# A step of context keys is dealt only after its staging buffer's last transfers were issued three rounds ago

## The chip, the core and the metric

One core of a Trainium2 chip runs the whole program. The metric is device time in microseconds (us) of one execution. Five engines have queues of their own and work through them in order: TensorE (PE in the profile, its weight loads PEld), VectorE (DVE), ScalarE (ACT), GpSimd (POOL) and SyncE (SP), which here issues nearly all transfers.

## The reference

Two layers of a transformer block work on `x` of shape (4, 512, 320), with a context of shape (4, 1601, 192):

```python
h1 = ln(x);  x = attn(h1, h1)  + x        # self attention, 20 heads of 16
h2 = ln(x);  x = attn(h2, ctx) + x        # cross attention, 1601 keys
h3 = ln(x);  a, g = split(h3 @ ff_w1 + ff_b1)
x = (a * gelu(g)) @ ff_w2 + ff_b2 + x     # 1280 hidden
# attn: softmax(q k' / 4) v, then the output projection wo and its bias
```

All of it is in float32.

## The kernel before

The work is cut into *units*: a batch element and a group of four heads for attention (20 units of self and 20 of cross attention in a layer), and one unit for each batch element of the feed-forward part. A unit of attention goes through its keys in *chunks* of 128: 4 chunks in a self unit, 13 in a cross unit. For a chunk PE makes the scores (`st`, L1187), subtracts the row maximum by one more product (L1190), ACT takes the exponential (L1200), and a chunk later PE multiplies by the values (`av`, L1214). The maxima come from products made ahead for the next unit (`sps`, L1011), which DVE reduces (L1030). Heads sit in slots of 32 rows, so that four small products run side by side in the array.

Beside this stream, filler work is dealt: normalisation, queries, keys, values, output projections, the turning of the context. Each kind has a chain, a queue in the planner's hands; an entry has a cost, a due round, a condition `ready` and a condition `soon`. A chunk is two *rounds* of the planner's clock, and at the end of each chunk the function `steps` takes entries from the heads of the chains, in order of their due rounds, as long as a credit lasts. An entry whose `soon` is false holds up its chain, and the other chains go on. All this happens while the program is built; the chip sees fixed queues.

The keys of the context are made by `keys_of_context(i)`, a *key step*: four PSUM banks (`kps`, L873) are filled by PE, two are copied by ACT and two by DVE (L882) into a staging buffer that lies in the tile `w2` (`w` or `w_109` in the views), POOL splits the result into a high and a low part (L697, L698), and SP issues the transfers that spread it over the rows of `kT` (`kT<-w`, L893 and L889). There are two such staging buffers, `kstage`, used in turn. `slots_soon` queues a step's transfers for the rounds that follow; if a buffer is asked for again before they were issued, `empty` issues them at once. A key step is 24 merged rows of products for one pair of units, or 48 smaller ones for a single unit; there are 80 key steps.

Nothing in the planner asks whether the transfers out of a buffer have gone when the next key step for it is dealt. The copies at L882 then carry that wait in the queues of ACT and DVE.

## Time and profile before

| | us |
|---|---|
| median of 3 runs | 3103.72 (3101.41 to 3106.84) |
| the profiled execution | 3100.62 |
| its span, first to last instruction | 3098.8 |
| PE busy | 2966.7 (96%) |
| DVE busy | 2192.6 (71%) |
| ACT busy | 1963.5 (63%) |
| POOL busy | 1269.3 (41%) |

The span is the stretch in which instructions ran; the execution's own time is 1.8 us longer. Ends of products are modelled, so PE's busy share tells little by itself; the idle time in front of an instruction and the name of what ended it tell more. In the rows of the views, `L882` is line 882 of the kernel, `xN` a count, and in a list of waits stand the total in us, the number of waits and the longest. The mean granted TensorE clock was 0.986 of full speed.

### The profile page before, as it was taken

How to read it: one execution, taken by the hardware profiler on the slowest of the kernel's cores; microseconds unless marked ns; L12 is line 12 of the kernel's file. 1: busy time of each engine (PE TensorE's matmuls, PEld its weight loads, DVE VectorE, ACT ScalarE, POOL GpSimd, SP SyncE). 2: the span in 40 equal slices, each digit the busy share in tenths (PEclk: the TensorE clock that was granted, in tenths of full speed). 3: DMA queues.
4: the chain of work that ended last, by engine and by line, in shares of the span. 5: the costliest groups of instructions: out<-in, count | busy, mean ns of one | idle time of the engine just before them, and what ended most of it. 6: DMA issues, size and time to landing. Idle time of an engine off the chain costs nothing.

```text
span 3098.8 us, 93413 instructions
## 1 busy us (share of the span) xinstructions
PE 2966.7 (96%) x37842; PEld 1615.6 (52%) x37842; DVE 2192.6 (71%) x4315; ACT 1963.5 (63%) x4029; POOL 1269.3 (41%) x1451
## 2 busy tenths in 40 slices
PE   8999999999999999999998999999999999999999
PEld 4455555554554555455554555555555555544555
DVE  7787888778778778522258888888888888884221
ACT  3677568777777778711137775778778778884110
POOL 3445335544544544311125553455555455442000
PEclk9999999999999999999999999999999999999999
DMA  4433221221221221300113332212211221112000
GB/s 104 103 69 80 55 47 41 59 46 34 59 46 33 58 42 22 88 6 1 28 36 84 73 69 48 44 46 42 42 46 35 41 57 35 31 25 67 9 13 13
DMA packets 213064, 145.35 MB, mean 47 GB/s; under 512 B 147476, under 2 KB 182680, under 8 KB 212632
## 3 DMA queue, kind: packets, MB, share of 16 engines
q1 hardware_dynamic: 211752, 138.32, 19.7%
q8 instruction: 297, 4.87, 0.7%
q10 hardware_dynamic: 880, 1.06, 0.1%
q14 instruction: 135, 1.11, 0.1%
HBM read 33.04 MB, written 7.93 MB: 13 GB/s over the span
## 4 chain that ended last, share of the span: by engine, by line
PE 70%; DVE 20%; DMA 2%; issue 2%; POOL 2%; ACT 2%; SPq 1%; ACTq 0%; POOLq 0%; DVEq 0%
PE av L1214 17%; PE st L1187 10%; DVE pm L1030 9%; PE fps L1309 9%; PE sps L1011 9%; PE yps L1364 6%; DVE nmax L1030 5%; PE ops L1126 3%; PE qps L797 3%; PE vps L965 3%; PE st L1190 3%; PE fps L1322 2%; PE kps L873 2%; PE vps L947 1%; DMA kT<-w 1%
## 5 line engine op out<-in xcount | busy, mean ns | idle before, releaser
L1030 DVE TENSOR_REDUCE pm<-sps 128x1 f32<-128x512 f32 x1920 | 1187.0, 679 | 86.1 <-PE sps L1011 79.3
L1011 PE MATMUL sps<-kT,q 32*128 32x512 f32 (+1 forms) x6400 | 1067.2, 406 | 26.5 <-DMA q<-stage 5.5
L1200 ACT ACTIVATE pr<-st 128x512 f32<-128x512 f32 (+1 forms) x1710 | 907.3, 603 | 216.1 <-PE st L1190 205.5
L1187 PE MATMUL st<-q,kT 32*128 32x512 f32 (+1 forms) x5440 | 943.8, 437 | 36.8 <-ACT w L882 27.3
L1231 POOL TENSOR_TENSOR o<-o,pr 128x512 f32<-128x512 f32 x359 | 462.0, 1287 | 694.4 <-ACT pr L1230 678.6
L1187 PEld LDWEIGHTS st<-q,kT 32*128 32x128 f32 (+1 forms) x5440 | 480.5, 181 | 395.6 <-ACT pr L1200 136.3
L1214 PE MATMUL av<-pr,vals 128*32 128x512 f32 (+1 forms) x3420 | 642.9, 614 | 37.6 <-DVE pm L1030 12.4
L1011 PEld LDWEIGHTS sps<-kT,q 32*128 32x128 f32 x6400 | 546.4, 185 | 137.2 <-DVE pm L1030 30.4
L1190 PE MATMUL st<-m,units 32*128 32x512 f32 (+1 forms) x2720 | 534.1, 393 | 2.8 <-DMA m<-turned 2.8
L1200 ACT ACTIVATE wself<-st 128x512 f32<-128x512 f32 (+1 forms) x867 | 464.3, 603 | 87.1 <-PE st L1190 81.5
L1030 DVE TENSOR_REDUCE nmax<-sps 128x1 f32<-128x512 f32 x640 | 395.6, 679 | 103.9 <-PE sps L1011 99.5
L1214 PE MATMUL av<-wself,vals 128*32 128x512 f32 (+1 forms) x1734 | 373.1, 612 | 12.9 <-DVE pm L1030 8.1
L1231 POOL TENSOR_TENSOR o<-o,wself 128x512 f32<-128x512 f32 x191 | 245.2, 1284 | 316.5 <-ACT wself L1230 316.4
L1332 ACT ACTIVATE pr<-fps,b 128x512 f32<-128x512 f32 x80 | 54.8, 687 | 373.5 <-PE fps L1322 266.1
L1309 PE MATMUL fps<-hT,w 128*128 128x512 f32 x640 | 285.0, 597 | 0.0
L1190 PEld LDWEIGHTS st<-m,units 32*128 32x128 f32 (+1 forms) x2720 | 251.4, 182 | 21.9 <-issue 2.7
L1230 ACT COPY pr<-av 128x512 f32<-128x512 f32 x359 | 218.9, 610 | 29.9 <-PE av L1214 29.0
L1214 PEld LDWEIGHTS av<-pr,vals 128*32 128x32 f32 (+1 forms) x3420 | 91.7, 108 | 207.0 <-DVE pm L1030 102.4
L1309 PEld LDWEIGHTS fps<-hT,w 128*128 128x128 f32 x640 | 118.5, 190 | 149.4 <-issue 147.2
L697 POOL TENSOR_SCALAR stage<-stage 128x256 fp32r<-128x256 f32 (+1 forms) x155 | 106.9, 689 | 172.2 <-ACT stage L808 87.5
L873 PEld LDWEIGHTS kps<-ctxT,w 32*128 32x128 f32 (+1 forms) x4992 | 113.6, 160 | 51.6 <-ACT pr L1200 23.1
L500 POOL TENSOR_SCALAR root<-root 128x4 f32<-128x4 f32 x23 | 5.2, 224 | 323.7 <-DVE root L494 323.3
(101 smaller groups left out, 3282.7 us busy)
## 6 DMA issues: line engine op xcount, KB each, us to landing
q<-stage SPq DMA_DIRECT2D x314, 128.0 KB
kT<-w SPq DMA_DIRECT2D x240, 104.0 KB
aT<-o SPq DMA_DIRECT2D x320, 32.0 KB
kT<-stage SPq DMA_DIRECT2D x156, 64.0 KB
kT<-w SPq DMA_DIRECT2D x80, 72.0 KB
w<-in_L_xattn_ff_w_dram SPq DMA_DIRECT2D x20, 256.0 KB
m<-turned SPq DMA_DIRECT2D x318, 4.0 KB
ctxT<-ctxT SPq DMA_DIRECT2D x24, 208.0 KB
```

Of the source, the lines that this page charges most:

```text
L697: eng.tensor_scalar(high.bitcast(F32R), x, 1.0, None, ALU.mult)
L873: see(nc.tensor.matmul(ps[to : to + n, :PIECE], lhsT=wk_q[rows, k, u.g * GD : u.g * GD + n], rhs=first.kvT[rows, k, at : at + PIECE], star ...
L1011: see(nc.tensor.matmul(out, lhsT=u.q[rows, t // 2, e, t % 2 * P : (t % 2 + 1) * P].bitcast(F32R), rhs=u.kT[rows, keys].bitcast(F32R), star ...
L1030: see(nc.vector.tensor_reduce(to[:, j : j + 1], ps, AX.X, ALU.max, negate=(ns == 1)))
L1187: see(nc.tensor.matmul(st[:r, :], lhsT=keys, rhs=u.q[rows, :, e].bitcast(F32R), start=(e == 0), stop=False))
L1190: see(nc.tensor.matmul(st[:r, :], lhsT=units_of[rows, :r].bitcast(F32R), rhs=u.mrow[rows, :].bitcast(F32R), start=False, stop=True,))
L1200: see(nc.scalar.activation(p[:r], st[:r], AF.Exp))
L1214: see(nc.tensor.matmul(ps[j * SLOT : (j + 1) * SLOT, :], lhsT=columns_of[:r, head : head + SLOT], rhs=pr.pop((c, j))[:r, :], start=True, s ...
L1230: see(nc.scalar.copy(vo, ps))
L1231: nc.gpsimd.tensor_tensor(u.o, u.o, vo, ALU.add)
L1309: see(nc.tensor.matmul(ps, lhsT=w1[:, k, i * FF + c * P : i * FF + (c + 1) * P], rhs=u.hT[:, k, :], start=ahead and k == 0, stop=not ahead ...
L1364: see(nc.tensor.matmul(ps[:, :D], lhsT=hid[c][:, t * P : (t + 1) * P], rhs=w2[:, c, :], start=(c == 0), stop=(c == NHC - 1),))
```

## The change

Two lists are added. `asked` counts how often a staging buffer was asked for, and `sent` notes the round in which the last transfer of each step was issued. The new condition `room` holds for a key step when the step before the last one, which used the same buffer, has all its transfers issued and three rounds have gone by. It is given to the key steps of the cross units as their `soon`. The ordinary staging buffer, which queries and the keys of self units use, only keeps count.

```diff
     groups = {"stage": deque(), "kstage": deque()}
+    sent = {"stage": [], "kstage": []}
+    asked = {"stage": 0, "kstage": 0}
+
+    def room(kind):
+        n = asked[kind] - 2
+        return n < 0 or len(sent[kind]) > n and clock["round"] >= sent[kind][n] + 3
...
     def stages(kind="stage"):
         empty(kind, 1)
+        asked[kind] += 1
...
         def last():
             done()
+            sent[kind].append(clock["round"])
...
-                add(chain, 1.1, lambda i=i: keys_of_context(i), keys_due - after, free)
+                add(chain, 1.1, lambda i=i: keys_of_context(i), keys_due - after, free, lambda: room("kstage"))
```

No instruction is added or taken away: the same work stands in another order. Of the 80 key steps, 21 were dealt in the round in which the last transfer out of their buffer was issued, and 5 two rounds after it; now 28 are dealt four rounds after, and none earlier (entries are taken at even rounds here, so three becomes four). The scores, the maxima and the rounds in which they stand do not move. The other filler entries move, since the planner deals them into the places that came free.

The first place is ACT's queue in the first cross unit of the second batch element, in the first layer. The four copies of the two key steps that come first, then the exponentials, then the next key step's copies. Before:

```order
L882 COPY w_109<-kps 128x104 x4
L1200 ACTIVATE wself<-st 128x512 x3
L1200 ACTIVATE pr<-st 128x512
L1230 COPY pr<-av 128x512
L882 COPY w_109<-kps 128x104 x2
L1200 ACTIVATE pr<-st 128x512 x4
L1225 COPY o<-av 128x512
L882 COPY w_109<-kps 128x104 x2
```

In ACT's queue of the new kernel, from the same four copies on (its lines are 8 higher):

```order
L890 COPY w_109<-kps 128x104 x4
L1208 ACTIVATE wself<-st 128x512 x3
L1208 ACTIVATE pr<-st 128x512
L1238 COPY pr<-av 128x512
L1208 ACTIVATE pr<-st 128x512 x4
L1233 COPY o<-av 128x512
L981 COPY vals<-vps 128x12x16 x2
L1208 ACTIVATE pr<-st 128x512
L1208 ACTIVATE wself<-st 128x512 x3
L1238 COPY wself<-av 128x512
L890 COPY w_109<-kps 128x104 x2
```

The third key step's copies moved from one chunk after the first two to three chunks after them.

The second place is PE's queue one batch element later, at the last of the four key steps. Before, the key step (`kps`) is alone between the values (`av`) and the next scores:

```order
L1214 MATMUL av<-pr,vals 32x512 x2
L1214 MATMUL av<-wself,vals 32x512 x2
L873 MATMUL kps<-ctxT,w_107 128x104 x24
L1187 MATMUL st<-q_92,kT_86 128x512 x2
L1011 MATMUL sps<-kT_89,q_93 128x512 x2
```

In PE's queue of the new kernel, two chunks later, a step of queries (`qps`) has come into the same place:

```order
L1222 MATMUL av<-pr,vals 32x512 x4
L881 MATMUL kps<-ctxT,w_107 128x104 x24
L805 MATMUL qps<-hT,w_109 32x128 x12
L1195 MATMUL st<-q_92,kT_86 128x512 x2
L1019 MATMUL sps<-kT_89,q_93 128x512 x2
```

The key step and the queries, which stood in two chunks, now share one. Twelve key steps stand so in the new order, with queries or values beside them that divide the array in another way; over the whole queue PE changes the division 1544 times instead of 1524.

The third place is SP's queue at the first of these places. Before, the transfers of the third key step stand ahead of those of a finished unit's output (`aT<-o`):

```order
L893 DMA kT_87<-w_109 64x4x104 x2
L893 DMA kT_89<-w_109 64x4x104 x2
L893 DMA kT_87<-w_109 64x4x104 x2
L1117 DMA aT<-o 16x512 x4
L893 DMA kT_89<-w_109 64x4x72
```

In SP's queue of the new kernel:

```order
L901 DMA kT_87<-w_109 64x4x104 x2
L1125 DMA aT<-o 16x512 x4
L901 DMA kT_89<-w_109 64x4x104 x2
L901 DMA kT_87<-w_109 64x4x104 x2
L901 DMA kT_89<-w_109 64x4x72
```

The output's transfers now stand ahead of the third key step's; this happens in about ten units.

## The prediction

> **What bounds the kernel now.** I read the page first, then the groups by line for the idle time ahead of each, then the waits of PE and ACT, and last the order of time around one wait.

> ```profile
> span 3098.8 us, 93413 instructions
> PE 2966.7 (96%) x37842; PEld 1615.6 (52%) x37842; DVE 2192.6 (71%) x4315; ACT 1963.5 (63%) x4029; POOL 1269.3 (41%) x1451
> PE 70%; DVE 20%; DMA 2%; issue 2%; POOL 2%; ACT 2%; SPq 1%; ACTq 0%; POOLq 0%; DVEq 0%
> ```

> PE is almost never idle and holds 70% of the chain that ended last: whatever lets PE stand still costs about its own length, and nothing else costs much. PE's idle time in the whole span is 3098.8 - 2966.7 = 132 us. The groups tell where some of it is:

> ```profile
> L1187 PE MATMUL st<-q,kT 32*128 32x512 f32 (+1 forms) x5440 | 943.8, 437 | 36.8 <-ACT w L882 27.3 <-DVE pm L1030 6.6 <-ACT pr L1200 1.5
> L882 DVE COPY w<-kps 128x104 f32<-128x104 f32 x160 | 34.5, 257 | 78.4 <-DMA kT<-w 44.7 <-PE kps L873 32.9
> L882 ACT COPY w<-kps 128x104 f32<-128x104 f32 x160 | 31.5, 249 | 96.6 <-PE kps L873 49.8 <-DMA kT<-w 43.7 <-issue 2.2
> ```

> The score products lose 27.3 us to the copies into the staging buffer, and those copies, short in themselves (249 and 257 ns), wait for the transfers out of it. As waits:

> ```profile
> PE st L1187 <- ACT w L882: 27.3, 15, 2.9
> PE av L1214 <- DVE pm L1030: 20.5, 28, 1.3
> PE st L1187 <- DVE pm L1030: 6.6, 9, 1.3
> PE sps L1011 <- DVE w L882: 4.9, 5, 1.0
> ACT w L882 <- DMA kT<-w: 43.7, 16, 3.8
> ```

> The largest single item of PE's idle time is the first line, and the count of 15 goes with the 16 of the last. One such wait in order of time, at the first place that the change's section shows:

> ```profile
> 634.89 0.39 ACT L882 COPY w<-kps 128x104 f32<-128x104 f32 x2 [0.72 <-PE kps L873]
> 636.82 10.81 SPq L893 DMA_DIRECT2D kT<-w  x12
> 638.48 1.62 PE L873 MATMUL kps<-ctxT,w 32*128 32x104 f32 x47
> 640.39 0.41 PE L1190 MATMUL st<-m,units 32*128 32x512 f32 x2
> 642.66 0.39 ACT L882 COPY w<-kps 128x104 f32<-128x104 f32 x2 [3.10 <-DMA kT<-w]
> 642.96 0.84 PE L1187 MATMUL st<-q,kT 32*128 32x512 f32 x2 [2.16 <-ACT w L882]
> 644.58 1.07 PE L1214 MATMUL av<-wself,vals 128*32 128x512 f32 x3
> 646.38 1.60 PE L873 MATMUL kps<-ctxT,w 32*128 32x104 f32 x48
> 647.74 0.48 PE L1187 MATMUL st<-q,kT 32*128 32x512 f32 x2
> ```

> The buffer is filled at 634.89, its transfers are issued from 636.82 on, and the next key step for the same buffer is on PE at 638.48. ACT reaches that step's copies and stands for 3.10 us until the transfers have landed at 642.66. The exponentials are queued behind the copies, the key step holds four of eight PSUM banks, so PE runs out of banks and stands for 2.16 us.

> **The change, part by part.** *The wait.* The change removes no work and adds none; DMA bytes, products and copies keep their counts. A key step now comes four rounds (two chunks) after its buffer's last transfers, where 21 steps came at no distance and 5 at two rounds. Of what is left at a distance of two rounds, the trace shows this:

> ```profile
> 2324.30 0.39 ACT L882 COPY w<-kps 128x104 f32<-128x104 f32 x2 [0.95 <-DMA kT<-w]
> 429.64 0.50 PE L1187 MATMUL st<-q,kT 32*128 32x512 f32 x2
> 432.07 0.84 PE L797 MATMUL qps<-hT,w 112*32 112x128 f32 x24
> 432.84 0.50 PE L1187 MATMUL st<-q,kT 32*128 32x512 f32 x2
> ```

> At two rounds the copy is at most 0.95 us late, with PE not idle at all. A chunk with one filler step takes 3.20 us (429.64 to 432.84), so two chunks push the copies at 642.66 at least 6.4 us from where ACT was ready for them (642.66 - 3.10 = 639.56), to 645.9 or later, 3.3 us after the landing. So I take the whole 27.3 us as gone: -27.3. The bounds are -27.3 and 0.

> What is queued behind the step that now waits in the planner: queries of the same chain, dealt two or so rounds later; the maxima that need keys and queries keep their rounds, and all of this slack is in the planner, not on an engine. The 4.9 us of `sps` behind DVE's copies belong mostly to steps that do not move, and I count 0.

> *The clock.* The wait at 640 to 643 leaves something behind:

> ```profile
> 642.90:646.40 3.50, 3.44 (x22) 1.19 (x22) 3.36 (x8) 2.23 (x6) 2.32 (x2) 0.52 0.57 119
> 553.00:556.00 3.00, 2.15 (x14) 1.05 (x18) 2.30 (x6) 1.98 (x6) 2.48 (x3) 0.68 0.76 218
> 789.00:793.00 4.00, 3.67 (x20) 1.36 (x21) 3.82 (x8) 2.70 (x7) 2.62 (x3) 0.58 0.01 5
> 876.00:880.00 4.00, 3.55 (x70) 2.34 (x74) 3.70 (x8) 2.98 (x7) 2.32 (x2) 1.00 0.46 96
> 1021.00:1025.00 4.00, 4.00 (x32) 2.17 (x32) 3.16 (x6) 2.64 (x5) 3.61 (x4) 0.59 0.00 0
> ```

> The third figure from the right is the granted clock. After the wait that ended at 642.96 it is about half for the next 3.4 us, and the value products take 1.07 us; after others it is 0.68, 0.58 and 0.59 over the stretch shown; after the one at 876 it is 1.00. PE at half clock for 3.4 us loses up to 1.7 us, and four of them 6.8. But at 789 DVE is busy 3.82 of 4.00 us and sets the pace itself, so that not every stretch costs that; I count one in full and little for the rest. I take -2, bounds 0 and -6.8. [...]

> *Moved filler that divides the array in another way.* Twelve key steps now share their chunk with queries or values in another division. One such pair stands in the trace of before:

> ```profile
> 396.92 2.25 PE L965 MATMUL vps<-w,ctxT 32*128 32x128 f32 x48
> 399.10 0.63 PE L947 MATMUL vps<-w,tail 96*32 96x128 f32 x12
> 399.66 0.50 PE L1187 MATMUL st<-q,kT 32*128 32x512 f32 x2
> ```

> A step of 48 products of that kind followed by scores in the same division needs 1.36 us to the next start (646.38 to 647.74, the key step); here, followed by another division, it needs 2.18 (396.92 to 399.10). So a pair costs up to 0.8 us, and at least nothing, since the changes of division around each step existed before as well. 12 x 0.8 = 9.7 at most; I take the half, +5. [...]

> *Normalisation and context.* Both move by up to 20 rounds in several units. Where they stood together, DVE was late and PE stood still:

> ```profile
> 768.39 0.45 PE L1187 MATMUL st<-q,kT 32*65 32x512 f32 x2 [1.33 <-DVE pm L1030]
> 999.17 0.45 PE L1187 MATMUL st<-q,kT 32*65 32x512 f32 x2 [1.34 <-DVE pm L1030]
> ```

> In the new order the context's turning at these two places comes earlier and the normalisation later. Two waits of 1.3 us would go, and new ones of that kind may come where three steps of normalisation are now dealt at once (twice before in the cross units, twice now, elsewhere). The kind is 6.6 us in all; bounds -6.6 and +6.6; I take -3, the two waits.

> *POOL and SP.* POOL's splits move with the copies. POOL is busy 41% and its adds feed only the end of a unit: 0. On SP, the output's transfers now stand ahead of those of a third key step; that is the rival below. Inside the forecast: 0.

> The sum: -27.3 - 2 + 5 - 3 = -27.3. On the profiled execution (3100.6 with 1.8 us around its span) that gives 3073.3. The median of the runs shown is 3.1 us above that execution, so I predict 3076. With the good ends of all terms (-27.3 - 6.8 - 6.6 + 0 = -41) it is 3063, with the bad ends but the wait gone (-27.3 + 0 + 9.7 + 6.6 = -11) it is 3093.

> **The rivals.** *The wait stays (no change).* SP works in order, and a wait of its own holds up all behind it:

> ```profile
> SPq L1117 <- DVE pm L1030: 160.2, 28, 13.9
> ```

> Output transfers (L1117) wait for DVE up to 13.9 us, mean 5.7. If they now held up key transfers ahead of a copy, the copies would find the buffer full again. For it: they moved ahead in about ten units. Against it: what they moved ahead of is the third step's transfers, whose buffer is asked for again only in the next pair of units, some 40 rounds on. If it came about at most places: 3098 to 3110. Chance 0.06.

> *The gain is spent on the new order.* The pairs and the DVE meetings cost more than their rows: to bring it within 0.2% (6.2 us, about what a measurement here can tell from no change) the twelve pairs would need 1.8 us each instead of 0.4. The pair in the trace gives 0.8 at most. 3097 to 3110, chance 0.05.

> *Slower.* The twelve steps that take two kinds of filler hold five PSUM banks between values and scores, and ACT has three copies ahead of the next exponentials. If PE ran dry there as it does at 640 to 643, the wait would only have moved; to be slower than before by 0.2% it needs (27.3 + 6.2) / 12 = 2.8 us at each. The longest wait in the row of PE behind these copies is 2.9, so each would have to be as bad as the worst. It speaks against it that pairs stood before too, at seven places, and the longest wait on DVE's reductions is 1.3. At 3.5 us each: 3100.6 - 27.3 + 42 = 3115, 3118 as a median. Chance 0.04.

> *More than forecast.* The clock and the DVE meetings all go and pairs cost nothing: under 3063, about 3058. Chance 0.09.

> **How the numbers follow.** The forecast's own range, 3063 to 3093, has 0.76, and 3076 is its middle by the values taken. With the lower case reaching to 3060 the range 3060 to 3093 leaves out about 0.2. Faster by over 0.2%: 0.76 + 0.09 = 0.85, and 0.02 of the two cases near no change; same 0.09; slower 0.04.

> **What would show it.** In the profile after: the row of L882 without `DMA kT<-w` on either engine (88.4 us before); no row of `st` behind ACT's L882 above a few us; PE's idle time near 105 us instead of 132; the half clock gone at those four places; the pairs as chunks about 0.4 us longer than the sum of their parts. The forecast is wrong if ACT still waits for `kT<-w`, if a new line of some 20 us stands among PE's waits (by the slower rival behind L882 or L808 at the twelve pairs), or if PE's busy time grows by more than 10 us.

## The result and the profile after

| | before | after |
|---|---|---|
| median of the runs, us | 3102.88 (3101.41 to 3106.84) | 3058.98 (3052.44 to 3060.89) |
| ratio, 95% interval | | 0.9847 (0.9834 to 0.9859) |
| the profiled execution | 3100.62 | 3052.44 |
| PE idle in its span | 132.1 | 92.6 |
| lost to the clock, (1 - granted clock) x span | 43.4 | 21.4 |
| the rest: PE at work, at full clock | 2923.3 | 2936.6 |

The change saves 43.9 us where 27.3 were forecast, and 3058.98 lies just under the range. The last three rows of the table split the span into three parts; I read every run that follows by this split. The granted clock is given to 0.001, so the last two rows hold to some 1.5 us. The head of the page of the kernel after, with the chain of work that ended last as its last line:

```profile
span 3050.6 us, 93447 instructions
PE 2958.0 (97%) x37842; PEld 1611.9 (53%) x37842; DVE 2185.8 (72%) x4315; ACT 1959.4 (64%) x4029; POOL 1270.9 (42%) x1451
...
PE 70%; DVE 23%; issue 2%; ACT 2%; DMA 1%; POOL 1%; SPq 1%; ACTq 0%; DVEq 0%; POOLq 0%
```

PE's share of the chain is what it was; DVE's rose from 20 to 23%, and DMA's and POOL's fell by one each. Its row of cores, with the mean granted clock (0.986 before):

```profile
core 0: 3050.6 us, clock 0.993
```

The groups by line of the kernel after (its lines are 8 higher; busy time, then idle time ahead and what ended it):

```profile
L1195 PE MATMUL st<-q,kT 32*128 32x512 f32 (+1 forms) x5440 | 948.8, 437 | 5.2 <-DVE pm L1038 1.8 <-ACT pr L1208 1.5 <-DVE nmax L1038 1.0
L890 DVE COPY w<-kps 128x104 f32<-128x104 f32 x160 | 34.2, 255 | 50.4 <-PE kps L881 48.4 <-POOL o L1239 1.9
L890 ACT COPY w<-kps 128x104 f32<-128x104 f32 x160 | 31.5, 249 | 61.3 <-PE kps L881 56.7 <-issue 4.5
```

The score products lose 5.2 us instead of 36.8, and no copy waits for `kT<-w` any more (88.4 us before). That part went as forecast. PE's largest waits now (total, number, longest):

```profile
PE av L1222 <- DVE nmax L1038: 11.7, 27, 1.4
PE av L1222 <- DVE pm L1038: 11.2, 21, 1.6
PE sps L1019 <- DVE w L890: 8.2, 9, 1.0
...
PE st L1195 <- DVE pm L1038: 1.8, 4, 0.6
```

The waits for DVE's maxima (`pm`) fell too, from 20.5 to 11.2 and from 6.6 to 1.8; those behind DVE's copies, which the forecast held at 4.9, rose to 8.2. At none of the four places where the prediction saw half clock is any left: between 390 and 1570 us the trace after has no half clock at all. PE's idle time fell by 39.5 us, more than the wait's row; the loss to the clock fell by 22; PE's time at full clock rose by 13. Three things can therefore have made the gain larger than forecast: the wait itself, the new order, or the clock.

### The profile page after: what moved, and what is told of

Its sections match the earlier page's. It is cut to its first block, busy times and chain, and to the rows that moved or that the text cites. A ratio compares the mean times of both kernels' runs of the same rounds, so it can differ in the third digit from the quotient of the medians.

```text
span 3050.6 us, 93447 instructions
## 1 busy us (share of the span) xinstructions
PE 2958.0 (97%) x37842; PEld 1611.9 (53%) x37842; DVE 2185.8 (72%) x4315; ACT 1959.4 (64%) x4029; POOL 1270.9 (42%) x1451
## 4 chain that ended last, share of the span: by engine, by line
PE 70%; DVE 23%; issue 2%; ACT 2%; DMA 1%; POOL 1%; SPq 1%; ACTq 0%; DVEq 0%; POOLq 0%
PE av L1222 17%; DVE pm L1038 11%; PE st L1195 10%; PE fps L1317 9%; PE sps L1019 9%; PE yps L1372 6%; DVE nmax L1038 5%; PE ops L1134 3%; PE kps L881 3%; PE vps L973 3%; PE qps L805 3%; PE st L1198 2%; PE fps L1330 2%; PE vps L955 1%; PE kps L838 1%
## 5 line engine op out<-in xcount | busy, mean ns | idle before, releaser
L1222 PE MATMUL av<-wself,vals 128*32 128x512 f32 (+1 forms) x1734 | 369.8, 606 | 11.2 <-DVE pm L1038 5.9
L1222 PEld LDWEIGHTS av<-pr,vals 128*32 128x32 f32 (+1 forms) x3420 | 91.5, 108 | 196.6 <-DVE pm L1038 89.8
```

The source lines that it names most:

```text
L1222: see(nc.tensor.matmul(ps[j * SLOT : (j + 1) * SLOT, :], lhsT=columns_of[:r, head : head + SLOT], rhs=pr.pop((c, j))[:r, :], start=True, s ...
```

## The experiments

Ratios are to the kernel before on the same chip. In the first two expectations theory A says that the wait alone was worth about 46 us, theory B that it was worth its row (29 us with a stretch of half clock) and that the new order gave the rest.

### The wait without the order

Four staging buffers in the cross units instead of two, the order of every engine as before. A fourth buffer has room only where one of the 12 places for exponentials stood, so the cross units have 11.

```diff
-        "cross": mine + [wself[:, i * N : (i + 1) * N] for i in range(5)],
+        "cross": mine + [wself[:, i * N : (i + 1) * N] for i in range(4)],
...
-    kstage = [
-        [w2_flat[:, 3 * D + i * kw : 3 * D + (i + 1) * kw].rearrange("p (a w) -> p a w", a=4) for i in (j, j + 1)]
-        for j in (0, 2)
-    ]
+    ends = [w2_flat[:, 3 * D + i * kw : 3 * D + (i + 1) * kw] for i in range(5)]
+    ends += [w1_flat[:, (2 * KB + 2) * D : (2 * KB + 2) * D + kw]] + [wself[:, 4 * N + i * kw : 4 * N + (i + 1) * kw] for i in range(2)]
+    kstage = [[t.rearrange("p (a w) -> p a w", a=4) for t in ends[j : j + 2]] for j in range(0, 8, 2)]
...
-            kstage.reverse()
-            return kstage[0]
+            kept["i"] = (kept["i"] + 1) % (4 if at_place["kind"] == "cross" else 2)
+            return kstage[kept["i"]]
```

> The order of before, instruction for instruction on every engine, with four staging buffers for context keys in the cross units instead of two (and 11 instead of 12 places for the exponentials there). A key step's copies then find a buffer whose transfers were issued at least twelve rounds earlier, so the wait goes and nothing else moves. Theory A, the wait cost more than its row in the list of waits (the 12 stalled chunks shrank by 32.5 us between the two traces, their neighbours by 13.6): about 3057 us, no half clock behind the four places. Theory B, the wait cost its row plus one stretch of half clock (29.3 us) and the rest of the gain came from the new order (turning and normalisation met DVE elsewhere): about 3074 us. A rival to both: the copies also come late for another reason, and the time stays near 3103.

Measured: 3074.31 us, 0.9891 (0.9876 to 0.9906). That is theory B's number, but by accident. In this run and in the run "The order without the wait" the buffers were rotated by one list for all units, so the first six key steps of the second layer could take a buffer that lies over weights of the self units. That changes what the second layer computes, and adds waits there. The first line below is one that the order of before does not have; the second is one of the 15 waits, which stayed (at 412.9 us; the kernel before waits 2.05 us at 412.0):

```profile
PE vps L947 <- POOL wself L696: 3.1, 1, 3.1
PE st L1187 <- ACT w L882: 2.4, 1, 2.4
```

So I repeated it with a turn of its own for the self units (the diff above), which takes some 12 us off the time (0.9891 to 0.9852).

> Again the order of before with four staging buffers for the context keys in the cross units (and 11 places for the exponentials), the buffers now in turn so that those of the self units stay apart: in the first such run the first six key steps of the second layer could be given a buffer that lies over weights of the self units. The wait alone goes. Theory B (the wait at its row and one stretch of half clock, 29 us; the rest of the gain is the new order): PE idle near 105 us, av and st still wait 27 us or more for DVE's maxima, about 3074 us plus up to 5 for the places, so 0.990. Theory A (the wait at 46 us): 0.986 or less.

Measured: 3056.80 us, 0.9852 (0.9837 to 0.9868). The head of the page, then the row of cores:

```profile
span 3052.4 us, 93480 instructions
PE 2950.1 (97%) x37842; PEld 1612.0 (53%) x37842; DVE 2190.2 (72%) x4315; ACT 1963.9 (64%) x4029; POOL 1270.5 (42%) x1451
```

```profile
core 0: 3052.4 us, clock 0.992
```

The group of the scores, and the largest of PE's waits:

```profile
L1187 PE MATMUL st<-q,kT 32*128 32x512 f32 (+1 forms) x5440 | 941.1, 436 | 9.6 <-DVE pm L1030 6.5 <-ACT pr L1200 1.5 <-DVE nmax L1030 1.0
```

```profile
PE av L1214 <- DVE pm L1030: 20.5, 26, 1.4
```

The wait is gone and DVE's waits are as they were: `av` and `st` still wait for `pm` 20.5 and 6.5 us. The kernel is nevertheless 46 us faster. Idle time fell by 29.8 us (102.3 is left), close to the wait's row of 27.3; the time at full clock is that of before (2925.7 to 2923.3); and the loss to the clock fell from 43.4 to 24.4. The clock of every run is on record, not only that of the profiled one, and says the same: from the nine runs of the kernel before on this chip to the four of this one the mean loss falls from 48.9 to 29.0 us, by 20, and the span without the loss from 3052.9 to 3025.5, by 27. Theory B fell, and theory A's number was right: the part that goes beyond the wait's row shows as clock.

The control for the places:

> A control for the two runs with four buffers: the kernel before with 11 instead of 12 places for the exponentials in the cross units, nothing else. If the places do not matter: 3103 us, within 3. If they do, it is slower, and the runs with four buffers carry that too.

Measured: 3111.94 us, 1.0016 (1.0004 to 1.0028). So the run above may carry some 5 us (1 to 9) of the missing place. The split of this control is 133.2 idle, 49.7 clock, 2922.8 rest: the difference is in the clock again, not in PE's work. Over all its 12 runs the mean loss is 56.0 us, against 52.4 in the 17 runs of before on that chip, and the span without it 3053.5 against 3052.5. Whether that comes from the place or from the draw of the execution (below) I can't tell.

### The order without the wait

The changed kernel with the same four buffers:

> The changed kernel's order with the same four buffers. If four rounds are enough for the transfers, as the trace of after says (no copy waits for them), nothing changes: 3059 us, within 6. If the transfers still cost something that the list of waits puts under another name (the ordering on SP's queue, a copy that waits for several things), it is under 3050.

Measured: 3069.01 us, 0.9875 (0.9858 to 0.9892), with the second layer changed as in the first run above. That change alone made the order of before some 12 us slower, so this run can't say whether four buffers would gain anything on top of the new order. That nothing is left at the transfers rests on the profile after, where no copy waits for one. The changed kernel itself on the chip of the repeat:

> The changed kernel itself, as the measure for the other runs on this chip: 3059 us, ratio 0.985, within 0.002.

Measured: 3057.36 us, 0.9853 (0.9839 to 0.9866). The order of before with no wait (0.9852) and the changed order (0.9853) take the same time; the control leaves open that the changed order costs up to 9 us. No gain of the order shows. Its profile splits into 91.5 idle, 24.4 clock and 2938.6 rest, so the 10 us of idle time that it saves against the run with four buffers come back as 13 us in which PE counts as busy. Since the page models the ends of products, I take these two as one thing under two names: work that stood where PE waited now stands where PE is full.

The pairs, taken apart by ending a step's dealing where a key step would meet other filler:

```diff
             if cost >= 0.1:
+                if done and (cost == 1.1) != wide:
+                    break
+                wide = cost == 1.1
                 share = (2.2, 1.1) if beside else ...
```

> The changed kernel, but the planner ends a step's dealing where a key step would stand beside queries or values: none of the 16 such places is left (the 12 new ones and the 4 at the units that are prepared early); the key steps still come four rounds or more after their buffer's transfers. By the chunks of the trace of after the 12 pairs cost 11 us together: 3048. By the forecast's 0.4 us each: 3054. If the deals that are put off come back as other crowded chunks: 3059 or more.

Measured: 3059.80 us, 0.9847 (0.9831 to 0.9863), the changed kernel's own ratio; split 95.8 idle, 27.5 clock, 2932.6 rest. Taking the pairs away gains nothing that shows (the two ratios differ by 0.0006, and the intervals leave room for 8 us). My sum of 11 us from the chunks of the trace after was wrong: that a chunk is longer than its parts did not say what the same parts cost when they are dealt elsewhere.

Normalisation moved further than the prediction says. Four of the cross units' normalisations stand 86 to 88 rounds earlier (rounds 354 to 266 and 484 to 396 by their first entry; 1130 to 1044 and 1260 to 1174 by their third, the first two having stood at 1064 and 1194), not "up to 20". Two more move by one entry alone, so the count in the next expectation is off as well. `steps` ends when the entry that is due first lacks credit; a key step whose condition is false is passed over instead, and the planner goes on to light entries that are due much later. Two runs, theory C being that this is what emptied DVE's waits and gave 15 us:

```diff
-                (lambda: b == 0 or clock["round"] >= loaded[b] + 5) if t == 0 else yes,
+                (lambda: b == 0 or clock["round"] >= loaded[b] + 5 and clock["round"] >= due - 32) if t == 0 else yes,
```

> The changed kernel, but a normalisation may begin at the earliest ten rounds ahead of its due round, as it does in the order of before. In the changed kernel the planner, while it holds a key step back, deals further down its chains, and six normalisations of the cross units stand up to 96 rounds earlier, away from the turning of the context. Theory C (that move is what emptied the waits for DVE: 21 to 11 us on av, 6.6 to 1.8 on st): 12 to 16 us slower than the changed kernel, about 3074, with those waits back. If normalisation's place does not matter: 3059, as the changed kernel.

```diff
-                due = lead(u) - 10
+                due = lead(u) - (98 if u.cross and u.b else 10)
```

> The kernel before, two staging buffers and no new condition, but with the normalisations of the cross units from the second batch element on due 88 rounds earlier, where the changed kernel deals them. 21 key steps still come in the round in which their buffer's transfers are issued, so the wait behind ACT's copies stays at about 27 us. Theory C: 12 to 16 us faster than before, about 3088, with the waits for DVE halved. Otherwise: as before, 3103.

Measured: 3051.17 us, 0.9832 (0.9819 to 0.9846) for the changed kernel with normalisation held back, and 3115.24 us, 1.0037 (1.0025 to 1.0050) for the kernel before with normalisation early. Waits of the latter:

```profile
PE st L1187 <- ACT w L882: 31.2, 15, 4.6
PE av L1214 <- DVE pm L1030: 12.9, 15, 1.4
```

Theory C fell, with the sign turned. Moving normalisation early did cut the wait for `pm` from 20.5 to 12.9, and the kernel became some 12 us slower; holding it back made the changed kernel 6 us faster, though its waits for DVE add up to about what the changed kernel's do:

```profile
PE av L1222 <- DVE pm L1038: 7.1, 17, 1.3
...
PE st L1195 <- DVE pm L1038: 4.8, 8, 1.3
```

The second run does more than its expectation says: its edit moves all six normalisations of the later batch elements, so also the two of the second batch element (`hn` made from 436 us on instead of 531 in the first layer), which the changed kernel leaves nearly where they were. Why the early place costs, beyond 4 us more at the copies and 10 us more of PE's time at full clock (2933.0), stays open.

### The clock

The granted clock in the traces is either full or half (1.0 or 0.5). In 14 profiles (all runs here and the two kernels) there are 204 runs of half clock of 3.41 us or a multiple; within one execution each begins at a whole multiple of 3.4133 us after the first, to 0.005 us. Cut at these points, the span falls into stretches of 3.413 us. Here are three of them around the wait that the prediction showed, and three around a longer wait, the one at 876 us, in windows of the kernel before (length, busy time of PE, PEld, DVE, ACT and POOL, then granted clock, DMA share, GB/s):

```profile
639.43:642.84 3.41, 1.36 (x36) 0.93 (x31) 0.16 (x1) 0.31 (x3) 2.11 (x2) 1.00 0.60 125
642.84:646.25 3.41, 3.29 (x18) 1.17 (x18) 3.30 (x7) 2.29 (x6) 2.32 (x2) 0.50 0.56 117
646.25:649.66 3.41, 3.41 (x76) 2.53 (x76) 1.93 (x6) 1.93 (x5) 0.75 (x1) 1.00 0.53 110
871.53:874.94 3.41, 2.08 (x58) 1.64 (x55) 0.52 (x1) 0.85 (x2) 2.76 (x3) 1.00 0.63 131
874.94:878.35 3.41, 1.90 (x18) 0.75 (x18) 2.15 (x6) 2.20 (x6) 1.48 (x2) 1.00 0.47 97
878.35:881.76 3.41, 3.41 (x76) 2.54 (x76) 3.21 (x9) 2.19 (x7) 1.94 (x2) 1.00 0.44 92
```

The wait of 2.16 us lies almost whole in the first stretch, which has 2.05 us without PE; the next stretch is granted half. The wait of 2.84 us is cut in two by the boundary at 874.94, 1.33 and 1.51 us, and the clock stays full. So of these two the shorter wait, which leaves one stretch idle for 2.05 us, is followed by half clock, and the longer one, with at most 1.51 us in a stretch, is not. Theory D: a wait costs its idle time and, where 1.8 us or more of it fall in one stretch (all 64 stretches with 1.82 us or more in the last table are followed by half clock), up to 1.7 us more, half of 3.413. To test it I left the wait and took away the idleness, with products that nothing reads behind the 15 key steps whose copies wait (`STALLED`).

```diff
+            if (clock["round"], i) in STALLED:
+                for k in range(3):
+                    nc.tensor.matmul(pss[3][:, 128:], lhsT=ident, rhs=first.kvT[:, k, : 512 - 128], start=True, stop=True)
             high, low = stages("kstage")
```

> The kernel before, with three extra products (128 rows by 384 columns, about 0.45 us each by the 597 ns of 512 columns in the feed-forward part, 1.35 us together) behind each of the 15 key steps whose copies wait, written into a free part of one of the step's own banks; nothing reads them. The copies wait for the transfers as before. Theory D: a wait costs its idle time and then half clock, because PE stood idle for 1.8 us or more inside one stretch of 3.41 us; with products in it no such stretch is left there, so PE's idle time at these places falls from 27 to about 7 us, the half clock in the cross stages from 34 us to 14 to 20, and the time falls by 8 to 12 us although work was added: about 3093, 0.997. Rival: the half clock there follows from something else (the transfers themselves, the rush behind the wait): it stays, and the time is that of before, 3103, or up to 20 us more where the products do not fit into the waits.

Measured: 3094.84 us, 0.9965 (0.9953 to 0.9977). From the page, the row of cores, and the group of the products:

```profile
PE 2993.0 (97%) x37932; PEld 1631.0 (53%) x37932; DVE 2194.1 (71%) x4315; ACT 1962.2 (63%) x4029; POOL 1269.2 (41%) x1451
```

```profile
core 0: 3094.9 us, clock 0.988
```

```profile
L884 PE MATMUL kps<-ctxT,ident 128*128 128x384 f32 x90 | 33.0, 503 | 0.0
```

The same place in order of time, then the two stretches around it in this execution:

```profile
642.55 2.20 PE L884 MATMUL kps<-ctxT,ident 128*128 128x384 f32 x6
644.56 0.39 ACT L887 COPY w<-kps 128x104 f32<-128x104 f32 x2 [2.60 <-DMA kT<-w]
644.68 0.50 PE L1192 MATMUL st<-q,kT 32*128 32x512 f32 x2
```

```profile
641.43:644.84 3.41, 3.41 (x51) 2.23 (x48) 0.45 (x3) 0.81 (x4) 2.41 (x3) 1.00 0.62 128
644.84:648.25 3.41, 3.31 (x63) 1.94 (x67) 3.00 (x7) 2.65 (x6) 2.32 (x2) 1.00 0.58 119
```

The copy still waits 2.60 us for the transfers, but PE works meanwhile and the next stretch has the full clock. The groups of the copies show that they were not helped:

```profile
L887 DVE COPY w<-kps 128x104 f32<-128x104 f32 x160 | 35.1, 258 | 78.2 <-DMA kT<-w 37.9 <-PE kps L875 31.4 <-PE kps L884 4.4
L887 ACT COPY w<-kps 128x104 f32<-128x104 f32 x160 | 31.5, 249 | 95.7 <-PE kps L875 46.3 <-DMA kT<-w 36.7 <-ACT o L1230 4.9
```

The products took 2.20 us for three (0.73 us each, not the 0.45 that I had estimated), 33.0 us in all, and so filled the waits completely. 33 us of useless work took the place of 26 to 30 us of idle time, the engines stood idle ahead of the copies as long as before (78.2 and 95.7 us, against 78.4 and 96.6; some of it now put down to the products), and the time fell by 11 us (7 to 15), within theory D's 8 to 12. No work and no wait of the copies went, only half clock: over its 12 runs the mean loss is 31.7 us, against 50.2 in the 17 runs of before on that chip. So that half clock cost some 11 us (7 to 15) or more.

> The kernel before itself, for one more profile. By theory D the waits repeat within 1 us (15 waits of PE behind ACT's copies, 27 to 28 us) but the half clock behind them does not, since the stretches of 3.41 us lie differently against the waits in each execution: anything from 20 to 65 us of half clock in the cross stages, and a time of 3098 to 3115 that goes with it. If the half clock belongs to the places, it is within a few us of the 34 us of the first profile.

Measured: 3110.89 us for the one run. From the page, the row of cores, and PE's wait:

```profile
PE 2981.0 (96%) x37842; PEld 1623.0 (52%) x37842; DVE 2190.9 (70%) x4315; ACT 1963.9 (63%) x4029; POOL 1269.1 (41%) x1451
```

```profile
core 0: 3109.1 us, clock 0.981
```

```profile
PE st L1187 <- ACT w L882: 25.8, 15, 2.6
```

The same 15 waits, 25.8 us; idle time 128.1 and rest 2921.9 as in the first profile, but 59.1 us lost to the clock instead of 43.4 (in the cross stages 61.4 us at half clock instead of 34.1, by the clock records of the traces). The first profile, on which my forecast rested, was a favourable draw: in the 43 runs of the kernel before on the three chips of the experiments the loss goes from 37 to 65 us, with a mean of 51.

These 43 runs show one thing more. From run to run on one chip, 1 us more of loss goes with 0.67 us more of time (0.56 to 0.77). So the loss as the split counts it is an upper price: about a third of it does not show in the time, and the 20 us that the clock gives in the run with four buffers are worth 13 to 20.

| | idle | clock | rest | half clock in the cross stages |
|---|---|---|---|---|
| before, two profiles | 132.1, 128.1 | 43.4, 59.1 | 2923.3, 2921.9 | 34.1, 61.4 |
| before, products in the waits | 101.9 | 37.1 | 2955.9 (33.0 added) | 20.5 |
| before, four buffers | 102.3 | 24.4 | 2925.7 | 13.7 |
| after, two profiles | 92.6, 91.5 | 21.4, 24.4 | 2936.6, 2938.6 | 3.4, 3.4 |

### Two rounds, and a better version

`+ 1` in place of `+ 3` in `room`:

> The changed kernel with one round instead of three after the last transfer, so that key steps come two rounds after it, a chunk earlier. The forecast said that at two rounds a copy is at most 0.95 us late and PE not idle: then no wait of PE behind ACT's copies above 2 us in all, and 3055 to 3062, as the changed kernel. If two rounds are too few at places: up to 27 us of the wait come back.

Measured: 3065.71 us, 0.9868 (0.9839 to 0.9897), not told apart from the changed kernel, though the median lies above the 3055 to 3062 expected: its four runs scatter from 3057 to 3076, with a loss to the clock of 27 to 52 us. The copies wait for no transfer; ACT's:

```profile
L890 ACT COPY w<-kps 128x104 f32<-128x104 f32 x160 | 31.5, 249 | 64.0 <-PE kps L881 47.6 <-POOL o L1239 5.7 <-issue 5.1
```

Three buffers, the condition asked of the step three back, normalisation held (of its diff, the condition):

```diff
-        n = asked[kind] - 2
+        n = asked[kind] - (3 if at_place["kind"] == "cross" else 2)
```

> An attempt at a better version: three staging buffers in the cross units, the new condition asked of the step three back, and the normalisation held to ten rounds ahead of its due round. Key steps come four rounds or more after their buffer's transfers, and only five places are left where one stands beside queries or values or normalisation in the cross units (twelve in the changed kernel). If both the wait and the crowded chunks cost what the runs so far say: 3045 to 3052. If the new order costs nothing, as the equal times of the two orders without waits say: 3052 to 3058.

Measured: 3062.72 us, 0.9857 (0.9836 to 0.9878): no better than the changed kernel, and outside both of the expected ranges; why was not tried. The best of all runs is the changed kernel with normalisation held to ten rounds ahead (0.9832): its four runs, 3048.38 to 3053.83, lie below all four of the changed kernel on that chip, 3056.03 to 3059.26, though the intervals of the two ratios still touch.

## Why the prediction was wrong, step by step

- *The wait, -27.3.* Right. Without it, in the order of before, PE's idle time fell by 29.8 us; no copy waits for a transfer at four rounds or at two.
- *The clock, -2, bounds 0 and -6.8.* This is the step that failed. Measured: 11 us (7 to 15) or more by the products in the waits, and a mean loss that falls by 20 us with four buffers and by 21 with the change (runs on one chip), of which some two thirds, 13 and 14 us, or more shows as time. Two errors made it small. I counted only the four stretches of half clock that I had looked at, though the mean granted clock of 0.986 said 43 us for the span. And I took the one profile for the kernel, while the loss changes from execution to execution (37 to 65 us). That a stretch in which DVE is busy costs less than 1.7 us was not wrong in kind, by the 0.67 above; that it costs next to nothing was never measured. The bound of -6.8 set the lower end of the range: with 13 to 20 us for this term and the others as they stood the sum is -38 to -45, and the median 3065 to 3058.
- *The pairs, +5.* Not seen: without them the time is the same to within 8 us. The bounds 0 and 9.7 held as far as that tells. The price of 0.8 us compared unlike steps: the 48 products in the row at 396.92 have 128 columns, those of the key step 104.
- *DVE's meetings, -3 within 6.6.* The waits fell by 14 us, outside the bounds, and no gain of it shows: PE's time at full clock rose by 13. The bounds were the row of `st` alone, while the row of `av`, 20.5 us, stood in the same list; and I had normalisation moving by 20 rounds, and it moved by 88.
- *POOL and SP, 0.* Not tried by itself. The profile after shows no copy that waits for a transfer, which is the wait that SP's new order could have brought back.
- *The rivals.* None of the mechanisms of "the wait stays", "spent on the new order" and "slower" came about. "More than forecast" had the number, about 3058, and in part its reasons: the half clock at the four places went and the pairs cost nothing that shows. The number was luck all the same: its terms at their best add up to -41, which gives 3063.

## What to carry to other kernels

## What the hardware did that I had not expected

Of the stretches of 3.413 us at full clock in the 14 profiles, by PE's idle time inside the stretch:

| idle in the stretch, us | stretches | followed by half clock |
|---|---|---|
| 1.82 or more | 64 | 64 |
| 1.4 to 1.82 | 61 | 34 |
| 1.0 to 1.4 | 206 | 20 |
| under 1.0 | 11938 | 86 |

What set off the 86 in the last row, among them five of the eight runs of half clock in the profile after, was not tried. The traces have a hint. In 82 of these 86 stretches 15 to 25 products start, by the records, and in only some 450 of the 11852 others of that row; 56 of the 86 lie between 340 and 410 us or between 1860 and 1950, where the self units pass into the cross units. So PE may have less to do there than its busy time says, since the ends of products are modelled; the rows above count idle time alone and miss that.
